# Attention with a fused feed-forward gate: activations of the scores by head, and the two heads' subtractions of the maximum on either side of the next scores and maxima

## The chip, the cores and the metric

The kernel runs on one core of a Trainium2 chip. A core has engines that run side by side, each through its own list of instructions in order, and that wait for each other by semaphores: PE (TensorE, matrix products into PSUM; PEld are its weight loads), ACT (ScalarE, activations), DVE (VectorE), POOL (GpSimd) and SP (SyncE, which here issues the DMA transfers). PSUM holds results of PE in eight banks of 512 fp32 values per partition; SBUF is the working memory. The metric is the device time of one launch in microseconds (us).

## The reference

Eight batches of 2048 tokens of 512 channels. Each token is normalized (xn); attention with eight heads of 8 query/key and 64 value channels is taken of it; a feed-forward part with a base matrix and a routed low-rank part gives a gate; the two are multiplied and added to the input.

```python
q = (x @ Wq.T + bq).reshape(B, M, H, dqk)      # x here is xn
k = (x @ Wk.T + bk).reshape(B, M, H, dqk)
v = (x @ Wv.T + bv).reshape(B, M, H, dv)
scores = jnp.einsum('bmhd,bnhd->bhmn', q, k) / math.sqrt(dqk)
scores = jnp.where(scores >= 0, scores, 0.2 * scores)
beta = jax.nn.softmax(scores, axis=-1)
out = jnp.einsum('bhmn,bnhd->bmhd', beta, v).reshape(B, M, C)
s = gamma * out + x
g = silu(ffn(xn))                              # base + the chosen low-rank expert
return x_in + s * g
```

The maximum that softmax subtracts can be taken before the leaky step, since that step keeps the order; the kernel does so.

## The kernel before, in words

Work is split into 8 batches x 4 pairs of heads x 4 blocks of 512 queries = 128 stages (`s`). In each stage a loop of 16 steps (`i`, CH = 16) goes over the keys in chunks of 128, so the main loop has 2048 steps. A score tile `sc` has 128 keys on partitions and, for each of the pair's two heads `e`, 512 queries: two PSUM banks, one per head.

The order of all instructions on each engine is the order in which the program issues them (the schedule is written by hand); semaphores and waits between engines are derived from which tiles are written and read. One step of the main loop (L983 to L1027) issues:

1. `less_max` (L647): for both heads a matmul of two rows that adds minus the maximum (`shift`) to the score tile in place, on PE, at L652.
2. `score` (L630): for both heads the scores of the next step, L635, into the other of two score tiles.
3. `max_unit` (L570): for both heads the scores once more with queries on partitions, L585, for a stage ahead (25 steps ahead), into a single PSUM tile `mx` of two banks, and the DVE reduction to maxima, L592.
4. `exp` (L661): ACT's exponential of the score tile into one of seven SBUF buffers `ex`, L663.
5. `leaky` (L644): ACT's parametric relu, in place, on the next step's score tile, L645.
6. Filler: `background` (L802) issues pieces of three queues (the ending of the last stage, the maxima's transposition into shift rows, and the projections and gates of blocks to come), and `weigh` (L669) issues the weighted sums of one or two earlier steps, L675, four matmul records per step. What is issued when is fixed when the program is written out, by a count of PE's cost (`spent`) against due times.
7. `add_up` (L687): POOL adds `ex` into the sum of exponentials, L695, in 15 of 16 steps.

The small matmuls of 1 to 3 use 32 of PE's 128 rows each. `rows(r, e)` (L566) gives four groups of 32 rows: step `i` subtracts on the groups of `i % 2`, scores of the next step lie on the other two, and the maxima on `1 - kb % 2`, which is the pair that the subtraction uses. Matmuls on different groups can run at the same time.

The opening (to L977) normalizes and projects the first batch; L871 and L870 copy transposes there. Normalization of later blocks is L310 (ACT), the gate's tanh L513 (ACT), projections of queries and keys L257 and of values and the gate L271 (PE).

Of the kernel before, what the change touches and what calls it, by code (L numbers as in the profile page):

```python
# [11 lines left out]
AF = mybir.ActivationFunctionType  # L12
# [13 lines left out]
SLOPE = 0.2  # L26
# [6 lines left out]
def fused_layer_kernel(  # L33
# [37 lines left out]
    nc = tc.nc  # L71
# [3 lines left out]
    CH = NB * NT  # L75
# [4 lines left out]
    qscale = 1.0 / (DQK ** 0.5)  # L80
# [76 lines left out]
    ones_r = const.tile([128, 128], FR, name="ones_r")  # L157
# [367 lines left out]
    def where(s):  # L525
        return s // SEQ, s % NPAIR, (s % SEQ) // NPAIR
# [4 lines left out]
    shifts = {}  # L531

    def load_stacks(s):

        if s >= B * SEQ:
            return
        b, p, n = where(s)
        while b > 0 and b not in ready:
            background(force=True)
        q_sb = qp.tile([128, BLK], FR, name="q_sb")  # L540
        for r in range(2):
            half = slice(2 * STK * r, 2 * STK * (r + 1))
            nc.sync.dma_start(
                out=kst[s % 3][half, :].bitcast(FP).rearrange("r (c p) -> r c p", p=128),
                in_=KS[b][2 * p : 2 * p + 2].rearrange("e j d (c r p) -> r (e j d) c p", r=2, p=128)[r],
            )
        for r in range(2):
            half = slice(2 * STK * r, 2 * STK * (r + 1))
            nc.sync.dma_start(
                out=q_sb[half, :].bitcast(FP),  # L550
                in_=QS[b][2 * p : 2 * p + 2, :, :, n * BLK : (n + 1) * BLK].rearrange("e j d m -> (e j d) m"),
            )
        qst[s] = q_sb

    def load_values(s):
        if s >= B * SEQ:
            return
        b, p, n = where(s)
        while b not in valued:
            background(force=True)  # L560
        vts[s] = two.tile([128, CH, 128], FP, name="v_sb")
        nc.sync.dma_start(out=vts[s], in_=VS[b][p])
# [3 lines left out]
    def rows(r, e):  # L566
        g = 2 * r + e
        return slice(STK * g, STK * g + STK)

    def max_unit(s, u):  # L570

        if s >= B * SEQ:
            return
        if u == 0:
            mxr[s] = sm.tile([128, 2, NT, NB], FP, name="mxr")
        t, kb = u // NB, u % NB
        k_sb, q_sb = kst[s % 3], qst[s]
        if rooms:
            rooms.append(rooms.pop(0))
            mx = rooms[-1][0].tile([128, 2, BLK], FP, name="mx", tag=rooms[-1][1])  # L580
        else:
            mx = ps_x.tile([128, 2, BLK], FP, name="mx")
        for e in range(2):
            r = rows(1 - kb % 2, e)
            nc.tensor.matmul(  # L585
                mx[:, e, :],
                lhsT=q_sb[r, t * 128 : (t + 1) * 128],
                rhs=k_sb[r, kb // 2 * BLK : (kb // 2 + 1) * BLK],
                start=True,
                stop=True,  # L590
            )
        nc.vector.reduce_max(mxr[s][:, :, t, kb : kb + 1], mx, axis=AX.X)  # L592

    def shift_rows(s):
        if s >= B * SEQ:
            return
        m = sm.tile([128, 2 * NT, 1], FP, name="m")
        nc.vector.reduce_max(m, mxr.pop(s).rearrange("p e t n -> p (e t) n"), axis=AX.X)
        yield IDLE

        ml = sm.tile([128, 2 * NT], FP, name="ml")
        c = sm.tile([128, 2, 2 * NT], FP, name="c")
        big = sm.tile([128, 2 * NT], FP, name="big")
        nc.vector.tensor_scalar(big, m[:, :, 0], 0.0, SLOPE, ALU.min, ALU.mult)
        nc.vector.tensor_scalar_max(m[:, :, 0], m[:, :, 0], 0.0)  # L605
        nc.gpsimd.tensor_tensor(ml, m[:, :, 0], big, ALU.add)  # L606
        nc.gpsimd.tensor_tensor(big, ml, splitter.to_broadcast([128, 2 * NT]), ALU.mult)
        nc.gpsimd.tensor_tensor(ml, ml, minus_one.to_broadcast([128, 2 * NT]), ALU.mult)
        nc.gpsimd.tensor_tensor(c[:, 1, :], big, ml, ALU.subtract)
        nc.gpsimd.tensor_tensor(c[:, 0, :], big, c[:, 1, :], ALU.subtract)  # L610
        nc.gpsimd.tensor_tensor(c[:, 1, :], ml, c[:, 0, :], ALU.subtract)
        for _ in range(2):
            yield IDLE
        yield FREE
        cps = ps_m.tile([4 * NT, 128], FP, name="cps", tag="m")
        nc.tensor.transpose(cps, c.rearrange("p i m -> p (i m)"), ident)
        cT = sm.tile([4 * NT, 128], FP, name="cT")
        nc.vector.tensor_copy(cT, cps)
        spend(0.45)
        shift = qp.tile([128, BLK], FR, name="shift")  # L620
        for g in range(4):
            for i in range(2):
                o = 2 * NT * i + NT * (g % 2)
                nc.sync.dma_start(
                    out=shift[STK * g + i : STK * g + i + 1, :].bitcast(FP), in_=cT[o : o + NT, :]
                )
        shifts[s] = shift
        yield FREE

    def score(s, i):  # L630
        sc = ps_s.tile([128, 2, BLK], FP, name="sc")
        k_sb, q_sb = kst[s % 3], qst[s]
        for e in range(2):
            r = rows(i % 2, e)
            nc.tensor.matmul(  # L635
                sc[:, e, :],
                lhsT=k_sb[r, i // 2 * 128 : (i // 2 + 1) * 128],
                rhs=q_sb[r, :],
                start=True,
                stop=True,  # L640
            )
        return sc

    def leaky(sc):  # L644
        nc.scalar.activation(sc, sc, AF.Prelu, alpha=SLOPE)  # L645

    def less_max(s, i, sc):  # L647

        for e in range(2):
            r = rows(i % 2, e)  # L650
            r = slice(r.start, r.start + 2)
            nc.tensor.matmul(  # L652
                sc[:, e, :],
                lhsT=ones_r[r, :],
                rhs=shifts[s][r, :],
                start=False,
                stop=True,
                skip_group_check=True,
            )

    def exp(sc):  # L661
        ex = exq.tile([128, 2, BLK], FP, name="ex")
        nc.scalar.activation(ex, sc, AF.Exp, scale=qscale)  # L663
        return ex

    avt = {}
# [103 lines left out]
    def due_at(h):  # L770
        w, t = h * END, 0.0
        for _, _, _, cost, end in tasks:
            w += cost * max(0.0, min(1.0, (h - t) / (end - t)))
            t = end
        return w
# [62 lines left out]
    with tc.manual_schedule():  # L838
# [142 lines left out]
        sc0 = score(0, 0)  # L981
        leaky(sc0)
        for s in range(B * SEQ):  # L983
            for i in range(CH):
                if i == 0:
                    load_stacks(s + 2)
                if i >= 6 and s + 1 not in vts and (where(s + 1)[0] in valued or i == 13):
                    load_values(s + 1)
                due[0] = due_at(s + (i + 1) / CH)
                u = s * CH + i + CH + LEAD  # L990
                nxt = s * CH + i + 1
                less_max(s, i, sc0)
                if nxt < total:
                    sc1 = score(nxt // CH, nxt % CH)
                max_unit(u // CH, u % CH)
                if u % CH == CH - 1 and u < total:
                    queue[1], state[1] = shift_rows(u // CH), IDLE
                ex = exp(sc0)
                if nxt < total:
                    leaky(sc1)  # L1000

                begun = spent[0]
                k = 1
                if last and (slow[0] or last[0][1] == CH - 1):
                    slow[0] = False
                    k = 0
                    w = last.pop(0)
                    weigh(*w)  # L1010
                    background(most=0.8)
                    if spent[0] - begun < 0.4 and len(last) > 0 and w[1] < CH - 1:
                        k = 1
                else:
                    pairs = s < (B - 1) * SEQ
                    light = pairs and len(last) > 1 and (len(last) > MUCH or due[0] - begun < LATE)
                    background(pairs=pairs, light=light)
                    if spent[0] - begun > 1.5 and len(last) < 4:
                        k = 0
                    if spent[0] - begun < 0.4 and len(last) > 1 and last[0][1] < CH - 1:  # L1020
                        k = 2
                for w in last[:k]:
                    weigh(*w)
                del last[:k]
                add_up(s, i, ex)
                last.append((s, i, ex))
                sc0 = sc1  # L1027
# [48 lines left out]
```

## Time and profile before

| | us |
|---|---|
| median of 3 runs | 5808.57 (5797.81 to 5822.72) |
| profiled execution | 5811.92, span 5810.2 |
| PE busy | 5380.3 (93%) |
| POOL busy | 4783.6 (82%) |
| ACT busy | 4212.7 (73%) |
| DVE busy | 3656.9 (63%) |
| exponentials L663 | 2048, 1.023 each |
| parametric relus L645 | 2048, 1.020 each |
| additions L695 | 1920, 2.364 each |
| reductions L592 | 2048, 1.223 each |

The span runs from the first to the last instruction of the profiled execution. A line of the waits names who waited, for whom, the total in us, how often, and the longest. A line of the timeline gives the start, the duration, engine, line, operation, tiles and how many instructions are merged; in square brackets stands the idle time before it and who ended it. A line of the groups gives line, engine, operation, tiles and shapes, count, then busy us and mean ns of one, then idle time before and who ended it. The busy share of PE includes the modelled ends of pipelined matmuls. The granted PE clock was 0.966 over the span and 0.98 to 0.99 from 400 to 5000 us.

### The profile page before, as it was taken

The numbers are of one execution on the slowest core, as the hardware profiler recorded it, in microseconds if no ns is written. First come the engines' busy times: TensorE is split into PE (matmuls) and PEld (weight loads), VectorE is DVE, ScalarE is ACT, GpSimd is POOL, SyncE is SP. The second block draws the span as 40 slices with busy tenths as digits, with TensorE's granted clock in tenths as the row PEclk, the third lists the DMA queues.
The fourth block names the chain that finished last, engine by engine and source line by source line (L and its number), as shares of the span: only waits on it lengthen the run. The fifth ranks groups of instructions, "written<-read, shape, count | busy, mean of one in ns | idle before, by whom it ended". The sixth has DMA issues, their size and how long they took to land.

```text
span 5810.2 us, 74735 instructions
## 1 busy us (share of the span) xinstructions
PE 5380.3 (93%) x26386; PEld 1859.1 (32%) x26386; DVE 3656.9 (63%) x4972; ACT 4212.7 (73%) x4531; POOL 4783.6 (82%) x2904
## 2 busy tenths in 40 slices
PE   7899999999999999999999999999999999998898
PEld 3333333333333333333333333333333333333332
DVE  5566666666666666666666666666666666665553
ACT  2677767777777767777677776777767777776766
POOL 1788878888888878888788887888878888888877
PEclk9899999999999999999999999999999999998986
DMA  5324332343333333233432434224242243322221
GB/s 200 93 84 145 110 118 75 110 125 99 121 98 99 122 116 114 79 113 111 142 101 75 127 98 143 91 74 152 77 147 86 76 150 99 119 77 75 77 57 51
DMA packets 517996, 614.09 MB, mean 106 GB/s; under 512 B 30780, under 2 KB 429116, under 8 KB 481528
## 3 DMA queue, kind: packets, MB, share of 16 engines
q1 hardware_dynamic: 517624, 609.32, 34.6%
q8 instruction: 210, 3.44, 0.2%
q14 instruction: 162, 1.33, 0.1%
HBM read 405.79 MB, written 201.33 MB: 104 GB/s over the span
## 4 chain that ended last, share of the span: by engine, by line
PE 63%; ACT 23%; DVE 6%; issue 2%; POOL 2%; DMA 2%; SPq 1%; ACTq 0%; POOLq 0%; DVEq 0%
PE av L675 19%; PE sc L652 14%; ACT ex L663 11%; ACT sc L645 10%; PE zps L271 8%; PE vps L271 8%; PE mx L585 5%; PE qkps L257 2%; DVE mxr L592 2%; PE dps L257 2%; POOL acc L695 2%; PE pps L257 2%; DMA q_sb<-QS 1%; DVE bs L295 1%; PE sc L635 1%
## 5 line engine op out<-in xcount | busy, mean ns | idle before, releaser
L695 POOL TENSOR_TENSOR acc<-acc,ex 128x1024 f32<-128x1024 f32 x1792 | 4235.9, 2364 | 332.9 <-ACT ex L663 251.5
L592 DVE TENSOR_REDUCE mxr<-mx 128x2 f32<-128x1024 f32 x2048 | 2502.6, 1223 | 1593.3 <-PE mx L585 1576.5
L663 ACT ACTIVATE ex<-sc 128x1024 f32<-128x1024 f32 x2048 | 2095.9, 1023 | 1360.0 <-PE sc L635 1196.0
L675 PE MATMUL av<-ex,v_sb 128*64 128x512 f32 x8192 | 2170.2, 630 | 0.3
L645 ACT ACTIVATE sc<-sc 128x1024 f32<-128x1024 f32 x2048 | 2088.3, 1020 | 19.8 <-PE sc L635 19.8
L652 PE MATMUL sc<-shift,ones_r 2*128 2x512 f32 x4096 | 1057.1, 505 | 291.0 <-ACT sc L645 279.1
L652 PEld LDWEIGHTS sc<-shift,ones_r 2*128 2x128 f32 x4096 | 397.9, 185 | 2019.5 <-ACT sc L645 1949.1
L635 PE MATMUL sc<-q_sb,k 32*128 32x512 f32 x4096 | 1041.3, 505 | 0.0
L585 PE MATMUL mx<-k,q_sb 32*128 32x512 f32 x4096 | 832.7, 399 | 15.3 <-DVE mxr L592 11.1
L675 PEld LDWEIGHTS av<-ex,v_sb 128*64 128x64 f32 x8192 | 458.8, 138 | 809.3 <-issue 784.5
L695 POOL TENSOR_TENSOR acc<-ex 128x1024 f32<-128x1024 f32 x128 | 302.0, 2359 | 342.9 <-ACT ex L663 342.9
L271 PE MATMUL zps<-w_sb,xnT 128*128 128x512 f32 (+1 forms) x1120 | 541.7, 598 | 14.7 <-DMA xnT<-XT 10.7
L271 PE MATMUL vps<-wv_sb,xnT 128*128 128x512 f32 x960 | 481.7, 622 | 11.3 <-DVE lo L326 10.8
L585 PEld LDWEIGHTS mx<-k,q_sb 32*128 32x128 f32 x4096 | 402.4, 188 | 40.1 <-DVE mxr L592 32.1
L635 PEld LDWEIGHTS sc<-q_sb,k 32*128 32x128 f32 x4096 | 385.5, 185 | 0.8 <-issue 0.8
L271 PEld LDWEIGHTS zps<-w_sb,xnT 128*128 128x128 f32 x1120 | 188.5, 192 | 259.3 <-issue 193.9
L271 PEld LDWEIGHTS vps<-wv_sb,xnT 128*128 128x128 f32 x960 | 162.2, 189 | 223.5 <-issue 199.4
L514 DVE SCALAR_TENSOR_TENSOR g<-th,zps 128x512 f32<-128x512 f32 x128 | 88.0, 687 | 171.2 <-ACT th L513 171.2
L606 POOL TENSOR_TENSOR ml<-m,big 128x8 f32<-128x8 f32 x128 | 26.2, 205 | 167.2 <-DVE m L605 167.2
L257 PE MATMUL qkps<-xnT,wqk_sb 128*128 128x512 f32 x240 | 136.1, 703 | 7.5 <-DVE xnT L365 5.5
L257 PE MATMUL dps<-xnT,wd_sb 128*128 128x512 f32 (+1 forms) x280 | 141.1, 620 | 0.0
L257 PE MATMUL pps<-xnT,wp_sb 128*128 128x512 f32 (+1 forms) x280 | 133.3, 588 | 0.3
(124 smaller groups left out, 2627.5 us busy)
## 6 DMA issues: line engine op xcount, KB each, us to landing
v_sb<-VS SPq DMA_DIRECT2D x127, 1024.0 KB
k<-KS SPq DMA_DIRECT2D x256, 256.0 KB
XN<-xn SPq DMA_DIRECT2D x32, 1024.0 KB
q_sb<-QS SPq DMA_DIRECT2D x256, 128.0 KB
xnT<-XT SPq DMA_DIRECT2D x32, 1024.0 KB
GS<-g SPq DMA_DIRECT2D x32, 1024.0 KB
gs<-GS SPq DMA_DIRECT2D x128, 256.0 KB
xs<-in_x_dram SPq DMA_DIRECT2D x128, 256.0 KB
```

Source lines behind the costliest of these rows:

```text
L257: nc.tensor.matmul(ps[:, part], lhsT=wt[:, c, :], rhs=xnT[c][:, part], start=(c == 0 and part.start == 0), stop=(c == NC - 1 and part.stop ...
L271: nc.tensor.matmul(ps[:, part], lhsT=xnT[c][:, t * 128 : (t + 1) * 128], rhs=wt[:, c, part], start=(c == 0 and part.start == 0), stop=(c = ...
L295: nc.vector.bn_stats(bs, xt[:, t, :])
L514: nc.vector.scalar_tensor_tensor(g[:, t, :], th, 1.0, ps, ALU.add, ALU.mult)
L585: nc.tensor.matmul(mx[:, e, :], lhsT=q_sb[r, t * 128 : (t + 1) * 128], rhs=k_sb[r, kb // 2 * BLK : (kb // 2 + 1) * BLK], start=True, stop= ...
L592: nc.vector.reduce_max(mxr[s][:, :, t, kb : kb + 1], mx, axis=AX.X)
L635: nc.tensor.matmul(sc[:, e, :], lhsT=k_sb[r, i // 2 * 128 : (i // 2 + 1) * 128], rhs=q_sb[r, :], start=True, stop=True,)
L645: nc.scalar.activation(sc, sc, AF.Prelu, alpha=SLOPE)
L652: nc.tensor.matmul(sc[:, e, :], lhsT=ones_r[r, :], rhs=shifts[s][r, :], start=False, stop=True, skip_group_check=True,)
L663: nc.scalar.activation(ex, sc, AF.Exp, scale=qscale)
L675: nc.tensor.matmul(avt[s][64 * e : 64 * e + DV, :], lhsT=v_sb[:, i, 64 * e : 64 * e + DV], rhs=ex[:, e, :], start=(i == 0), stop=(i == CH ...
L695: nc.gpsimd.tensor_tensor(acc[s], old, ex, ALU.add)
```

## The change

The relu and the exponential are issued for each head's bank of the score tile, so ACT has four instructions of 128x512 in a step and not two of 128x1024. `less_max` takes the head as an argument. In a step the first head's subtraction is issued before the next scores and the maxima, and the second head's after them. Within the maxima of the main loop the second head now comes first (`flip`); the maxima that the opening issues keep their order. The amount of arithmetic, the transfers and the filler stay as they are.

```diff
-    def max_unit(s, u):
+    def max_unit(s, u, flip=False):
...
-        for e in range(2):
+        for e in (1, 0) if flip else (0, 1):
             r = rows(1 - kb % 2, e)
...
     def leaky(sc):
-        nc.scalar.activation(sc, sc, AF.Prelu, alpha=SLOPE)
-
-    def less_max(s, i, sc):
-
         for e in range(2):
-            r = rows(i % 2, e)
-            r = slice(r.start, r.start + 2)
-            nc.tensor.matmul(
-                sc[:, e, :],
...
+            nc.scalar.activation(sc[:, e, :], sc[:, e, :], AF.Prelu, alpha=SLOPE)
+
+    def less_max(s, i, sc, e):
+
+        r = rows(i % 2, e)
+        r = slice(r.start, r.start + 2)
+        nc.tensor.matmul(
+            sc[:, e, :],
+            lhsT=ones_r[r, :],
+            rhs=shifts[s][r, :],
+            start=False,
+            stop=True,
+            skip_group_check=True,
+        )
 
     def exp(sc):
         ex = exq.tile([128, 2, BLK], FP, name="ex")
-        nc.scalar.activation(ex, sc, AF.Exp, scale=qscale)
+        for e in range(2):
+            nc.scalar.activation(ex[:, e, :], sc[:, e, :], AF.Exp, scale=qscale)
         return ex
...
-                less_max(s, i, sc0)
+
+
+                less_max(s, i, sc0, 0)
                 if nxt < total:
                     sc1 = score(nxt // CH, nxt % CH)
-                max_unit(u // CH, u % CH)
+                max_unit(u // CH, u % CH, flip=True)
+                less_max(s, i, sc0, 1)
                 if u % CH == CH - 1 and u < total:
                     queue[1], state[1] = shift_rows(u // CH), IDLE
                 ex = exp(sc0)
```

More of the change, by code (lines that the diff above doesn't have):

```diff
@@ L644, in leaky @@
     def leaky(sc):
-        nc.scalar.activation(sc, sc, AF.Prelu, alpha=SLOPE)
-    def less_max(s, i, sc):
         for e in range(2):
-            r = rows(i % 2, e)
-            r = slice(r.start, r.start + 2)
-            nc.tensor.matmul(
-                sc[:, e, :],
[L654 to L659, printed above, removed]
+            nc.scalar.activation(sc[:, e, :], sc[:, e, :], AF.Prelu, alpha=SLOPE)
[10 more added lines that the diff above has]
+        )
     def exp(sc):
         ex = exq.tile([128, 2, BLK], FP, name="ex")
-        nc.scalar.activation(ex, sc, AF.Exp, scale=qscale)
+        for e in range(2):
+            nc.scalar.activation(ex[:, e, :], sc[:, e, :], AF.Exp, scale=qscale)
         return ex
```

## The prediction, made before the result

> **What bounds the kernel now.** I read the page first: the busy shares, then the chain that ended last.
>
> ```profile
> span 5810.2 us, 74735 instructions
> ...
> PE 5380.3 (93%) x26386; PEld 1859.1 (32%) x26386; DVE 3656.9 (63%) x4972; ACT 4212.7 (73%) x4531; POOL 4783.6 (82%) x2904
> ...
> PE 63%; ACT 23%; DVE 6%; issue 2%; POOL 2%; DMA 2%; SPq 1%; ACTq 0%; POOLq 0%; DVEq 0%
> ```
>
> PE looks full at 93%, but nearly a quarter of the chain is ACT, so some steps are set by ACT. Next, the waits (total us, times, longest us):
>
> ```profile
> PEld sc L652 <- ACT sc L645: 1949.1, 1988, 2.3
> ...
> ACT ex L663 <- PE sc L635: 1196.0, 1606, 3.8
> ...
> PE sc L652 <- ACT sc L645: 279.1, 615, 1.8
> ...
> PEld mx L585 <- DVE mxr L592: 32.1, 58, 1.8
> ```
>
> The subtraction (L652) waits for the parametric relu (L645); the exponential (L663) waits for the PE group that holds the subtraction: a circle. The timeline of one step, ACT first, then PE (start, duration), shows its size:
>
> ```profile
> 2502.31 1.02 ACT L663 ACTIVATE ex<-sc 128x1024 f32<-128x1024 f32 x1 [0.68 <-PE sc L635]
> 2503.23 1.02 ACT L645 ACTIVATE sc<-sc 128x1024 f32<-128x1024 f32 x1
> ```
>
> ```profile
> 2501.68 0.50 PE L652 MATMUL sc<-shift,ones_r 2*128 2x512 f32 x2
> 2501.69 0.50 PE L635 MATMUL sc<-q_sb,k 32*128 32x512 f32 x2
> 2502.03 0.39 PE L585 MATMUL mx<-k,q_sb 32*128 32x512 f32 x2
> 2502.63 0.27 PE L616 MATMUL cps<-ident,c 128*16 128x128 f32 x1 [0.21 <-DVE gs L742]
> 2502.82 1.08 PE L675 MATMUL av<-ex,v_sb 128*64 128x512 f32 x4
> 2504.30 0.50 PE L652 MATMUL sc<-shift,ones_r 2*128 2x512 f32 x2 [0.40 <-ACT sc L645]
> ```
>
> Subtraction to exp 0.62 us (median of all steps), exp to relu 0.92, relu 1.02, relu's end to the next subtraction 0.053: a circle of 2.61. PE needs less in this step and idles 0.40. From the instructions' starts over the 2047 steps of the main loop: 1486 begin within 0.08 us of the relu's end, with a period of about 2.617 (circle-bound); the other 561 are held by PE, DVE or a transfer. So most steps are circle-bound, though PE's own work in them (0.66 for the six small matmuls plus the filler at its shortest spacing) is often only a little shorter: 2.53 with eight weighted-sum matmuls (475 steps), 2.57 with four w or q/k projection matmuls (362), 1.6 to 2.05 with four weighted-sum matmuls alone, with the transpose of the maxima or with the denominators (381), about 2.26 with four plus some transposes or one projection matmul (187, and 74 that also normalize).
>
> **The change part by part.** *Two activations in place of each one.* 4096 more ACT instructions. The row of a 128x512 activation out of PSUM:
>
> ```profile
> L513 ACT ACTIVATE th<-zps 128x512 f32<-128x512 f32 x128 | 76.1, 595 | 29.9 <-PE zps L510 29.9
> ```
>
> 0.60 us, against 1.02 for 128x1024. Back to back, the next starts 0.10 before the end (exp to relu: 0.92 of 1.02; tanh to exp: 0.52 of 0.60). So a half is issued every 0.50 to 0.52; I take 0.505. Per step ACT has 4 x 0.505 = 2.02 instead of 2 x 0.92 = 1.84: 0.18 more, beside PE's work unless ACT is the circle. The bounds: 0.497 if the whole overlap holds, 0.60 if none does.
>
> The Trainium skill (ScalarE: Activation LUTs, What ACT_TABLE_LOAD costs) has a rule that speaks against the split: an activation with immediates pays 186 ns whatever its length, back-to-back ones overlap by about 93 ns, so each extra instruction costs some 93 ns. By it a half is issued every 0.52 us and four take 2.08, 0.06 more than mine; over the 642 steps that ACT would set below, the gain would be about 39 us smaller; paid without cover, the two extra instructions of all 2048 steps would be 381 us.
>
> *The first head's subtraction ahead, the second's behind.* The circle becomes that of one head: relu of head 0 ends, 0.053, subtraction, 0.62, exp of head 0, 0.505, exp of head 1, 0.505, relu of head 0, 0.60: 2.28 instead of 2.61. Head 1: its relu ends 0.505 after head 0's, so its subtraction starts 0.505 after the first, and its exp could start 1.125 after the first, just when ACT is free of head 0's (0.62 + 0.505). So it adds nothing. PE's six matmuls keep their count. Before, the four on both pairs of row groups start together and the two maxima 0.33 later. With the maxima flipped, second head first, the first four again lie on four row groups; maxima of head 0 and subtraction of head 1 form the second pair. I cost the reorder itself at nothing, hidden by that row-group concurrency; were it lost, 0.33 per PE-bound step.
>
> The added wait: head 1's subtraction waits for its relu with all following PE filler queued behind it. The relu of head 1 ends 2.74 after the subtraction of head 0 (0.62 + 3 x 0.505 + 0.60), and PE would reach the subtraction 0.34 after the next head-0 subtraction; it stalls when the period is under 2.79 - 0.34 = 2.45. A step with PE work W between then lasts (W + 2.45)/2.
>
> *The sum by kinds of circle-bound steps*, against 2.617:
> - 475 with W 2.53: 0.087 each, 41 us. 362 with W 2.57: 0.047, 17 us.
> - 381 with W up to 2.05: down to the circle, 0.334 each, 127 us.
> - 187 with W about 2.26: (2.26 + 2.45)/2 = 2.355, 0.262 each, 49 us.
> - 74 with a normalization (L310, 0.80, issued over 0.75) between relu and exp: ACT alone is 4 x 0.505 + 0.75 = 2.77, 0.16 more than now: 12 us lost.
>
> Together 222 us gained. Off it go two things. A short step leaves head 1's relu 0.17 late for the next (2.79 - 2.28 - 0.34); where the next is PE-heavy, which I put at 300 of the 381 (the planner follows a light step with a heavy one), that is 300 x 0.17 = 50 us. And the maxima: their buffer is single, and a maximum matmul waits for the DVE reduction (1.23) of the one before. The reduction ends 0.95 (median) before the next maxima start, but under 0.4 in 154 steps, where PE or DVE already waits. The flipped maximum is now in the first wave, 0.33 earlier, ahead of head 1's subtraction: 154 x 0.2 = 31 us. In the 568 short steps 0.95 shrinks by 0.33 (order) and 0.33 (period) to 0.29; a quarter of reductions start 0.34 or more late (0.77 against 0.43 after the maxima), so 142 x 0.2 = 28 us. I take 60, between 0 (all absorbed by head 1's wait for its relu) and 568 x 0.33 = 190 (every short step given back). What is late next is thus DVE's reduction, then PE.
>
> Net: 222 - 50 - 60 = 112. The profiled execution took 5811.9 (span 5810.2 and 1.7 around it), 0.06% over the median of 5808.57. 5812 - 112 = 5700.
>
> *What costs nothing.* POOL's addition (L695, 2.364) needs both halves of exp, which end 1.73 after the first subtraction instead of 1.64; seven ex buffers cover 0.09, and POOL's 15 in 16 steps average 2.2, under any mean period here. If that cover went, ACT would wait for buffers, now 30 us in all. SP and POOL queues are moved past nothing: no DMA changes place. The 561 other steps gain nothing.
>
> **The rivals.**
> *A. The wait stays whole* (slower). If the dependency of a subtraction on the relu, or of the exp on the subtractions, is kept for the two-bank tile and not for each bank, both subtractions wait for the second relu and both exps for the second subtraction, now 0.34 behind: 0.053 + 0.34 + 0.62 + 3 x 0.505 + 0.60 = 3.13 per step. It decides from one shared wait on. 1486 x 0.5 = 740 and 158 for the others: 5812 + 900 = 6710. For it: two engines reading different columns of one bank already take turns (the relay L870, L871 in the opening). Against it: the first weighted sum starts at 137.77, 1.25 us after the load of the last quarter of v_sb, which it doesn't read, was begun.
> *B. The halves don't overlap* (0.60 each). The circle is 2.47, but head 1's relu ends 3.02 after the subtraction, so stalls begin under 3.07 - 0.34 = 2.73: the heavy kinds gain nothing, the short 568 gain 0.15 (85 us), 74 normalizing steps lose 0.5 (37), PE-bound steps under 2.73 and followers lose about 70, DVE takes 60: 5812 - 85 + 37 + 70 + 60 = 5894. Exp to relu speaks against it.
> *C. It is given back.* DVE's end of its bound, 190, with the 50: 222 - 240, about no change, 5830.
> *D. All of it arrives:* no follower loss and no DVE loss: 5590.
>
> **How the numbers follow.** Forecast (5590 to 5780, D in it) 0.63; C 0.14, half of it within 0.5%; B 0.11; A 0.08; 0.04 for other losses. The range 5600 to 5895 reaches over C and B. 0.5%, about what a measurement of this kernel can tell from no change (its three runs lie 0.43% apart), is 29 us. Faster 0.66 (the forecast and a little of C), same 0.10, slower 0.24.
>
> **What the profile after would show.** Exp and relu groups of 4096 at 0.60; subtraction waits on relu much below 1949; short steps at 2.28, those with eight weighted sums at 2.53; an exp of head 0 starting 0.62 after its subtraction. Wrong would be: head 0's subtraction starting only after head 1's relu (A), halves issued every 0.60 (B), waits of the maxima on the reduction far above 43 us (C), or six small matmuls that take more than 0.66.

## The result

The changed kernel takes 6936.36 us (median; 6925.11 to 6956.84), against 5815.65 for the kernel before: a ratio of 1.1935, with a 95% interval of 1.1887 to 1.1982. The forecast was 5700, in a range of 5600 to 5895. The change made the kernel 19% slower, and the prediction was wrong, on the side of its rival A.

These lines of the changed kernel's page give the busy shares and the chain that ended last. ACT now has 55% of the chain, where it had 23%, and PE's busy share fell from 93% to 84%:

```profile
span 6923.3 us, 78741 instructions
...
PE 5796.0 (84%) x26386; PEld 1984.3 (29%) x26386; DVE 3672.3 (53%) x4972; ACT 4659.7 (67%) x8627; POOL 4771.8 (69%) x2904
...
ACT 55%; PE 37%; issue 4%; POOL 2%; DVE 1%; DMA 0%; ACTq 0%; SPq 0%; POOLq 0%; DVEq 0%
```

The waits (total us, times, longest us). The subtraction's wait for the relu (now L646), which was to shrink from 1949, grew, and so did the idle time of PE itself (from 279):

```profile
PEld sc L652 <- ACT sc L646: 2748.8, 1913, 2.7
...
ACT ex L664 <- PE sc L652: 1665.3, 1678, 9.3
...
PE sc L652 <- ACT sc L646: 1019.6, 1728, 2.3
```

One step in the timeline of the changed kernel, PE and then ACT (start, duration, instructions merged):

```profile
2999.62 0.50 PE L652 MATMUL sc<-shift,ones_r 2*128 2x512 f32 x1 [0.77 <-ACT sc L646]
2999.62 0.50 PE L635 MATMUL sc<-q_sb,k 32*128 32x512 f32 x2
2999.63 0.73 PE L585 MATMUL mx<-k,q_sb 32*128 32x512 f32 x2
2999.96 0.40 PE L652 MATMUL sc<-shift,ones_r 2*128 2x512 f32 x1
3000.29 1.08 PE L676 MATMUL av<-ex,v_sb 128*64 128x512 f32 x4
3002.73 0.79 PE L652 MATMUL sc<-shift,ones_r 2*128 2x512 f32 x1 [1.36 <-ACT sc L646]
```

```profile
3000.49 1.08 ACT L664 ACTIVATE ex<-sc 128x512 f32<-128x512 f32 x2 [0.92 <-PE sc L652]
3001.45 1.22 ACT L646 ACTIVATE sc<-sc 128x512 f32<-128x512 f32 x2
```

Three things stand in it. The first exponential starts 0.87 us after the first subtraction, not 0.62: 0.53 after the second one. The next first subtraction starts 0.05 after the end of both relus, not after the first. And the two relus take 1.22, since the second starts 0.637 after the first (median over all steps), when the first has ended, where the two exponentials take 1.08 and start 0.493 apart. So the circle, in medians over all steps, is 0.053 (relu's end to subtraction) + 0.867 (to the first exponential) + 0.493 (to the second) + 0.477 (to the first relu) + 0.637 (to the second) + 0.582 (its length) = 3.11, and 3.11 is the median distance of the steps (2.62 before); 1807 of 2048 steps start within 0.08 us of the second relu's end.

The semaphores in the trace say the same. In all 2048 steps the first subtraction signals nothing; only the second one updates the semaphore that the first exponential waits for.

### The profile page after: what moved, and what is told of

The parts are those of the page before. It is cut to its first block, busy times and chain, and to the rows that moved or that the text cites. A ratio compares the mean times of both kernels' runs of the same rounds, so it can differ in the third digit from the quotient of the medians.

```text
span 6923.3 us, 78741 instructions
## 1 busy us (share of the span) xinstructions
PE 5796.0 (84%) x26386; PEld 1984.3 (29%) x26386; DVE 3672.3 (53%) x4972; ACT 4659.7 (67%) x8627; POOL 4771.8 (69%) x2904
## 4 chain that ended last, share of the span: by engine, by line
ACT 55%; PE 37%; issue 4%; POOL 2%; DVE 1%; DMA 0%; ACTq 0%; SPq 0%; POOLq 0%; DVEq 0%
ACT ex L664 28%; ACT sc L646 27%; PE sc L652 16%; PE mx L585 7%; PE av L676 5%; PE zps L271 2%; PE qkps L257 1%; POOL acc L696 1%; PE vps L271 1%; PE dps L257 1%; PE tp L362 1%; ACTq L664 0%; DVE mxr L592 0%; PE dps L719 0%; DVE xnT L365 0%
## 5 line engine op out<-in xcount | busy, mean ns | idle before, releaser
L664 ACT ACTIVATE ex<-sc 128x512 f32<-128x512 f32 x4096 | 2222.9, 595 | 1995.9 <-PE sc L652 1665.3
L652 PE MATMUL sc<-shift,ones_r 2*128 2x512 f32 x4096 | 1642.7, 477 | 1027.2 <-ACT sc L646 1019.6
L646 ACT ACTIVATE sc<-sc 128x512 f32<-128x512 f32 x4096 | 2433.3, 594 | 84.3 <-PE sc L635 19.8
L676 PE MATMUL av<-ex,v_sb 128*64 128x512 f32 x8192 | 2313.7, 667 | 0.0
L585 PE MATMUL mx<-k,q_sb 32*128 32x512 f32 x4096 | 1551.3, 470 | 3.0 <-DVE mxr L592 3.0
L652 PEld LDWEIGHTS sc<-shift,ones_r 2*128 2x128 f32 x4096 | 685.5, 199 | 2937.5 <-ACT sc L646 2748.8
L635 PE MATMUL sc<-q_sb,k 32*128 32x512 f32 x4096 | 1095.2, 531 | 0.0
L585 PEld LDWEIGHTS mx<-k,q_sb 32*128 32x128 f32 x4096 | 607.1, 197 | 10.4 <-DVE mxr L592 8.9
L271 PE MATMUL zps<-w_sb,xnT 128*128 128x512 f32 (+1 forms) x1120 | 598.7, 653 | 7.4 <-DMA xnT<-XT 7.4
L257 PE MATMUL dps<-xnT,wd_sb 128*128 128x512 f32 (+1 forms) x280 | 178.0, 762 | 0.0
```

The costliest lines, as they stand in the source:

```text
L257: nc.tensor.matmul(ps[:, part], lhsT=wt[:, c, :], rhs=xnT[c][:, part], start=(c == 0 and part.start == 0), stop=(c == NC - 1 and part.stop ...
L271: nc.tensor.matmul(ps[:, part], lhsT=xnT[c][:, t * 128 : (t + 1) * 128], rhs=wt[:, c, part], start=(c == 0 and part.start == 0), stop=(c = ...
L585: nc.tensor.matmul(mx[:, e, :], lhsT=q_sb[r, t * 128 : (t + 1) * 128], rhs=k_sb[r, kb // 2 * BLK : (kb // 2 + 1) * BLK], start=True, stop= ...
L635: nc.tensor.matmul(sc[:, e, :], lhsT=k_sb[r, i // 2 * 128 : (i // 2 + 1) * 128], rhs=q_sb[r, :], start=True, stop=True,)
L646: nc.scalar.activation(sc[:, e, :], sc[:, e, :], AF.Prelu, alpha=SLOPE)
L652: nc.tensor.matmul(sc[:, e, :], lhsT=ones_r[r, :], rhs=shifts[s][r, :], start=False, stop=True, skip_group_check=True,)
```

## The experiments

Theory 1 is that every wait between ACT and PE on the score tile covers the whole tile of two banks (rival A). Theory 2 is that the four shorter activations and the late second subtraction cost this much by themselves. Medians are compared with the kernel before on the same chip: 5804.1 us in the first four runs, 5808.32 in the last three.

### A score tile for each head

The changed kernel with two tiles of one bank in place of one of two banks. Nothing else in the loop changes; the opening keeps its own tiles, which are given up before the loop.

```diff
     def score(s, i):
-        sc = ps_s.tile([128, 2, BLK], FP, name="sc")
+        sc = [ps_h[0].tile([128, BLK], FP, name=f"sc{e}", tag=f"sc{e}") for e in range(2)]
...
-                sc[:, e, :],
+                sc[e],
```

> The changed kernel, with the score tile made as two tiles of one bank, one per head. Theory 1 (each wait between ACT and PE covers the whole two-bank tile: both subtractions wait for the second relu, both exponentials for the second subtraction, and the second relu for the first): with a tile for each head the waits come apart, the circle falls from the 3.11 us of the changed kernel to 0.053 + 0.62 + 0.49 + 0.48 + 0.58 = 2.23, the first exponential starts about 0.62 after the first subtraction (0.87 now), and the time is that of the recorded sum, 5640 to 5750 us. Theory 2 (the cost lies in the four shorter activations and the late second subtraction as such): nothing comes apart, 6850 to 7000 us.

Measured: 5678.28 us, 0.9774 of before (0.9746 to 0.9801). The timeline, PE and then ACT, of a short step:

```profile
2499.61 0.50 PE L655 MATMUL sc<-shift,ones_r 2*128 2x512 f32 x1
2499.62 0.49 PE L638 MATMUL sc<-q_sb,k 32*128 32x512 f32 x2
2499.62 0.72 PE L586 MATMUL mx<-k,q_sb 32*128 32x512 f32 x2
2499.96 0.39 PE L655 MATMUL sc<-shift,ones_r 2*128 2x512 f32 x1
2500.28 1.08 PE L679 MATMUL av<-ex,v_sb 128*64 128x512 f32 x4
2501.84 0.50 PE L655 MATMUL sc<-shift,ones_r 2*128 2x512 f32 x1 [0.48 <-ACT sc L649]
```

```profile
2500.21 1.08 ACT L667 ACTIVATE ex<-sc 128x512 f32<-128x512 f32 x2 [0.44 <-PE sc L655]
2501.18 1.09 ACT L649 ACTIVATE sc<-sc 128x512 f32<-128x512 f32 x2
```

The same six PE instructions and the same four of ACT now go round in 2.23 us. The first exponential starts 0.60 after the first subtraction, the two relus take 1.09 (0.515 apart), and the next subtraction starts 0.43 before the second relu's end at 2502.27. Here each subtraction signals, and each exponential has a wait of its own. Only the tiles differ, so theory 1 holds and theory 2 falls. This kernel does what the prediction took the change to do, and its time lies in the forecast's range.

### The activations alone, and the order alone

Activations by head with both subtractions in their old place:

```diff
                 less_max(s, i, sc0, 0)
+                less_max(s, i, sc0, 1)
                 if nxt < total:
                     sc1 = score(nxt // CH, nxt % CH)
-                max_unit(u // CH, u % CH, flip=True)
-                less_max(s, i, sc0, 1)
+                max_unit(u // CH, u % CH)
```

> Activations by head, but both subtractions ahead of scores and maxima as in the kernel before. Theory 1: the second relu waits for the first (0.64 apart and not 0.48), and the subtractions wait for the second; circle 0.053 + 0.62 + 0.49 + 0.48 + 0.64 + 0.58 = 2.86 against 2.61, so some 0.24 in 1486 steps and 0.1 in the 561 others: 5815 + 357 + 56 = about 6230 us. If the move of the second subtraction were the whole cause: 5800 to 5850 us.

And the new order with activations of the whole tile:

```diff
     def leaky(sc):
-        for e in range(2):
-            nc.scalar.activation(sc[:, e, :], sc[:, e, :], AF.Prelu, alpha=SLOPE)
+        nc.scalar.activation(sc, sc, AF.Prelu, alpha=SLOPE)
...
-        for e in range(2):
-            nc.scalar.activation(ex[:, e, :], sc[:, e, :], AF.Exp, scale=qscale)
+        nc.scalar.activation(ex, sc, AF.Exp, scale=qscale)
```

> Activations of whole tiles as before, but the second subtraction behind scores and maxima, and the maxima flipped. Theory 1: the exponential waits for the second subtraction, 0.35 behind the first and 0.52 long to the exponential: 0.053 + 0.87 + 0.92 + 1.02 = 2.86, about 6230 us as with the halves alone, and the two together make the 0.49 per step of the changed kernel. If the split of the activations were the whole cause: 5800 to 5850 us.

Measured: the activations alone 6298.05 us, 1.0850 (1.0828 to 1.0871), median step 2.84; the order alone 6369.71 us, 1.0969 (1.0944 to 1.0993), median step 2.87. Both lose, and what they add to a step adds up to the changed kernel's: 2.62 + 0.23 + 0.25 = 3.10. Both came 70 to 140 us over what was expected, and show part of what the changed kernel shows more of (below): their mean granted clocks are 0.941 and 0.939, where the kernel before has 0.966. The step of the activations alone, ACT:

```profile
3000.50 1.08 ACT L664 ACTIVATE ex<-sc 128x512 f32<-128x512 f32 x2 [0.65 <-PE sc L635]
3001.47 1.22 ACT L646 ACTIVATE sc<-sc 128x512 f32<-128x512 f32 x2
3003.34 1.09 ACT L664 ACTIVATE ex<-sc 128x512 f32<-128x512 f32 x2 [0.65 <-PE sc L635]
```

The pair of relus again takes 1.22 where one whole relu took 1.02, and the exponentials follow 0.65 after ACT fell idle (0.68 before): the splitting buys almost no earlier start, and adds 0.20 to the relus alone.

A step of the order alone, PE and then ACT; the exponential follows the second subtraction, not the first:

```profile
2879.10 0.49 PE L651 MATMUL sc<-shift,ones_r 2*128 2x512 f32 x1 [0.26 <-ACT sc L645]
2879.44 0.39 PE L651 MATMUL sc<-shift,ones_r 2*128 2x512 f32 x1
```

```profile
2879.97 1.02 ACT L662 ACTIVATE ex<-sc 128x1024 f32<-128x1024 f32 x1 [0.93 <-PE sc L651]
```

### A score tile for each head, in the old order

The first experiment's kernel with both subtractions ahead of scores and maxima.

> A score tile for each head and activations by head, but both subtractions ahead of scores and maxima. Theory 1: the waits come apart here too; the second subtraction waits for its relu, which ends 2.70 us after the first subtraction, with scores and maxima queued behind it, so a step with PE work W under 2.70 lasts (W + 2.70)/2: no gain in the steps with eight weighted sums, 0.25 in the 381 short ones, 0.13 in 187: 5815 - 120 = about 5700 us, 5680 to 5790. So the order is worth little beside the tiles. Theory 2: as the halves alone.

Measured: 5733.58 us, 0.9881 (0.9857 to 0.9905), as expected. The tiles bring the larger part of the gain, and the second subtraction behind scores and maxima brings another 55 us. The likely reason is that PE then has those four matmuls to do while the second relu runs: here the second subtraction starts within 0.08 us of its relu's end in 1394 steps, against 393 with the new order.

### Work that does nothing, in idle time

The changed kernel, whose circle is 0.49 us longer, should by its 1486 and 561 steps have come to rival A's 6710. It took some 225 us more. Its matmuls of a step are not all alike: in 242 of 2047 steps the first subtraction takes 0.79 us and not 0.50 (73 before). The windows of the changed kernel, a stretch with short and one with long matmuls (busy us of PE, PEld, DVE, ACT and POOL, then the granted PE clock):

```profile
2990.00:3000.00 10.00, 7.41 (x52) 2.81 (x52) 6.54 (x9) 8.23 (x15) 7.77 (x4) 1.00 0.00 0
3005.00:3012.00 7.00, 7.00 (x18) 2.20 (x20) 2.47 (x6) 3.39 (x7) 4.28 (x8) 0.50 0.84 310
```

The granted clock is 1.00 in one and 0.50 in the other; it fell at 3002.50, within the idle 1.36 us of the step shown above. Step by step against the kernel before, 195 steps grew by over 1 us, 327 us together. To test whether idle PE is the cause, the light steps got a weighted sum with zero weights (the lines that choose the steps are shown in part):

```diff
+    def weigh_nothing(s, i, ex):
+        for e in range(2):
+            nc.tensor.matmul(
+                avt[s][64 * e : 64 * e + DV, :],
+                lhsT=zeros,
+                rhs=ex[:, e, :],
+                start=False,
+                stop=False,
+            )
...
+                elif len(last[:k]) == 1 and spent[0] - begun < 0.6 and not w and 0 < last[0][1] < CH - 1:
+                    weigh_nothing(*last[0])
```

> The changed kernel with matmuls that do nothing in its light steps: where a step has one weighted sum and little else, a weighted sum with zero weights is added (0.86 us of PE, which is idle there for 0.5 to 1.4 us). Theory: about 230 us of the changed kernel's loss are not its circle but steps in which PE's matmuls take 0.79 and not 0.50 us, since PE was idle too long (granted clock 0.908 against 0.966); then the extra work makes the kernel faster, 6700 to 6860 us, with a clock over 0.93. Rival: those steps are long for buffers or POOL; then the extra work gains nothing, 6930 to 7000 us.

Measured: 6707.21 us, 1.1548 (1.1524 to 1.1571), with more work on PE: the page has 28982 matmuls instead of 26386. The granted clock over the span:

```profile
core 0: 6709.8 us, clock 0.976
```

It was 0.908 in the changed kernel. The idle time of PE before the subtraction, 1019.6 there, became:

```profile
PE sc L652 <- ACT sc L646: 673.8, 1530, 2.3
```

Steps with a 0.79 us subtraction fell from 242 to 49, and those that grew by over 1 us from 195 to 46. So of the 1121 us lost, about 229 (6936 - 6707) are the clock, which drops because the longer circle leaves PE idle, and 892 (6707 - 5815) are the circle. The division is approximate: the filled kernel has more work on PE, and its clock is above that of the kernel before (0.966), which has 73 such steps.

### The order of the two maxima

The first experiment's kernel without the flip.

```diff
-                max_unit(u // CH, u % CH, flip=True)
+                max_unit(u // CH, u % CH)
```

> The kernel with a score tile for each head, with the maxima in the old order (first head first). The prediction's price: the first four matmuls no longer lie on four row groups, the maxima start 0.33 later and the second subtraction 0.33 after them, 0.33 us more in every step that PE sets (some 1500): 5950 to 6200 us. If the order within the maxima is of no account: 5660 to 5700 us.

Measured: 5671.79 us, 0.9762 (0.9739 to 0.9784), the same as with the flip. The prediction's price for it, 0.33 us in every step that PE sets, was wrong. The instructions' starts show why: without the flip the first maximum lies on the row group of the first subtraction, and still starts 0.013 us after it; the next two of the six start at 0.336 and 0.350, and the filler at 0.668. With the flip these are 0.010, 0.336, 0.347 and 0.665. In both, the first four of the six start at once and the other two 0.34 later.

### Maxima in two tiles

The first experiment's kernel with the maxima, too, in a tile for each head, and two reductions of 512 columns in place of one of 1024.

```diff
-            mx = ps_x.tile([128, 2, BLK], FP, name="mx")
+            mx = [ps_h[1].tile([128, BLK], FP, name=f"mx{e}", tag=f"mx{e}") for e in range(2)]
...
-        nc.vector.reduce_max(mxr[s][:, :, t, kb : kb + 1], mx, axis=AX.X)
+            for e in (1, 0) if flip else (0, 1):
+                nc.vector.reduce_max(mxr[s][:, e, t, kb : kb + 1], mx[e], axis=AX.X)
```

> The kernel with a score tile for each head, and the maxima in two tiles too, each with its own reduction of 512 columns. If waits of the first-wave maximum on the reduction of both heads cost what the prediction put on them (60 us), 5610 to 5660 us; two reductions for one add about 0.16 us of DVE per step, beside other work. If DVE's time itself is near the limit: 5690 us or more.

Measured: 5645.27 us, 0.9727 (0.9697 to 0.9756), the fastest kernel of this study, 2.7% under the kernel before. The intervals of this and of the first experiment overlap, and the two ran on different chips, so the 0.5% between them is likely, not certain. With one tile the maxima's wait for the reduction was, by the waits of the first experiment:

```profile
PEld mx L586 <- DVE mxr L593: 64.3, 117, 1.8
...
PE mx L586 <- DVE mxr L593: 24.8, 72, 1.0
```

and with two tiles:

```profile
PEld mx L586 <- DVE mxr L597: 49.8, 141, 0.5
```

The longest wait fell from 1.8 to 0.5 us, though DVE works 122 us more (3764.3 against 3642.3 on the pages).

## Why the prediction was wrong, point by point

**The step that failed** is "The circle becomes that of one head". It took for granted that the wait of a subtraction on a relu, and of an exponential on a subtraction, would be drawn for the one bank it touches. They are drawn for the tile: the circle became 3.11 and not 2.28. The prediction had the right question in rival A, and gave it a chance of 0.08 on evidence that does not reach it: the weighted sum that started before the last quarter of v_sb could have landed shows waits by part of a tile in SBUF, and nothing in the profile before showed two engines on two banks of one PSUM tile. With no such row, A's chance should have been far above 0.08, and the range should have held 6710.

**What the whole wait did to the rest.** With it, the move of the second subtraction is not hidden but delays both exponentials by 0.25 us, and the split of the relu isn't hidden either: the second half waits for the first to end (0.637 apart, not 0.505). The 1486 steps that were bound by the circle, most of which were to gain, grew by 921 us together, the clock's part included.

**Rival A's size.** Its circle, 3.13, was measured as 3.11. Its time, 6710, left out one term: the clock of a PE that idles longer. The run with filled idle time, 6707, is close to rival A's price without that term; the changed kernel is at 6936 with it. In that run the 1486 steps grew by 765 us (740 in the rival's sum) and the 561 others by 136. The sum had 158 for these without a working, so that the total came within 3 us is partly luck.

**The sum itself,** tried on the kernel in which the waits do come apart: 112 us were forecast and 126 measured (5804.1 - 5678.28). Its parts were less good than their total, so this nearness is partly luck. By the matmuls of a step, grouped as in the prediction and among those that lasted under 2.7 us before, the mean change was: steps with eight weighted sums -0.06 us (forecast -0.087); short steps -0.26 (-0.33 from the circle, which measured 2.23 for 2.28), the middle kind -0.11 (-0.26), normalizing steps +0.03 (+0.16), and steps with four projection matmuls +0.09 (-0.047). The last row, 37 us in 392 steps, lies in 76 of them that follow a short step. In 26 of these the first maximum had to wait for the reduction and started 0.39 to 1.22 us late; they grew by 33 us together, 24 of it in nine in which the clock also fell to 0.50. One of the nine:

```profile
2922.79 0.50 PE L655 MATMUL sc<-shift,ones_r 2*128 2x512 f32 x1 [0.27 <-ACT sc L649]
2924.00 0.50 PE L586 MATMUL mx<-k,q_sb 32*128 32x512 f32 x2 [0.71 <-DVE mxr L593]
2924.73 3.56 PE L272 MATMUL zps<-w_sb,xnT 128*128 128x512 f32 x4
```

The other 50 grew by 7 us, most of them by 0.2 each, with the second subtraction 0.05 behind its late relu. That is the lateness which a short step hands on and which the sum had as one term of 50 us. The halves' spacing, 0.505 in the sum, was 0.493 between two exponentials, 0.477 from an exponential to a relu and 0.515 between two relus.

**The Trainium skill's rule against the change** (ScalarE: Activation LUTs, What ACT_TABLE_LOAD costs: a fixed cost for each activation, about 93 ns of it overlapped) comes near where the instructions follow each other freely: 0.493 and 0.515 measured for the 0.52 estimated by it. It doesn't cover the pair of relus on one tile, 0.637.

**The reorder at no cost** held once the waits were apart, but not for the reason given: which row group comes first among the maxima had no part in it.

**The reduction as "late next"** was right in kind. On separate score tiles the maxima wait 89 us in all where they waited 43. The term was 60 us, and taking the shared tile away brought 33 (5678.28 - 5645.27; the two were not run together, and by their ratios it is 27). The 43 are 32.1 of weight loads, shown in the prediction, and this line of the kernel before:

```profile
PE mx L585 <- DVE mxr L592: 11.1, 45, 1.0
```

## What to carry to other kernels

Before two halves of a tile are handed to different engines for an overlap, make them two tiles, or find a row that shows that waits are drawn for less than the tile; here the same instructions ran 19% slower with one tile and 2% faster with two. In a circle of two engines, an instruction that is split or moved pays its fixed costs for certain, and gains only if each half releases its own successor. And where a longer wait leaves PE idle, its clock adds to the price: look at the granted clock of the stretch, not only at the length of the wait.

## What the runs showed of the hardware that was not expected

The PE clock fell to 0.50 without a long idle stretch. In the changed kernel 79 stretches of steps with slow matmuls begin; the longest PE gap in the 6.8 us before each was 1.35 us at the median, and after the first 160 us of the span no gap was over 1.63 us (by the modelled ends of the matmuls). The Trainium skill (TensorE: Matmul & The Clock Gate, Why this matters for your kernels) advises to have no idle gaps over about 3 us; here the clock fell with shorter ones, though not after each of them: 251 gaps were over 1 us. The clock records of this trace change every 3.41 us or at multiples of it. After the first 160 us PE was idle for 1.35 us at the median (0.36 to 2.16) in the 3.41 us before the clock fell, in one gap or several, and for 0.50 (0 to 1.68) where it stayed at 1.00. These ranges overlap, so the trace doesn't settle what sum of idle time decides. It does show what the return looked like: in all 154 cases PE had no idle time in the 3.41 us before it.

Two matmuls on the same 32 rows, the first subtraction and the first maximum in the kernel without the flip, started 0.013 us apart by the profile's records, hardly later than on different rows (0.010). In both orders it is the fifth of the six that starts 0.34 us after the first. What sets this was not tried.

An activation whose result is written in place into one half of a PSUM tile delayed the next one on the other half until its own end (0.637 apart, with the first 0.606 long), while on two tiles the pair overlapped (0.515 apart). So this, too, goes with the shared tile and is no limit of the engine.
